# Routing and scattering tokens beside the attention, and running the experts over groups of 7, 7 and 2 batches in one pass

## The chip, the core and the metric

The kernel runs on one core of a Trainium2 chip. The metric is device time in microseconds, from one launch to its end. The core has five engines that work through queues of their own: TensorE (PE, matmuls and transposes), VectorE (DVE), ScalarE (ACT), GpSimd (POOL) and SyncE (SP, which here only issues DMAs). An engine executes its queue in order; semaphores make it wait for another engine or for a DMA.

## The reference

A transformer block over 16 batches of 512 tokens of width 128: causal attention with 16 heads of 8, and then a mixture of 160 experts of which every token uses 8. Each batch has its own shift, scale and gate vectors (`sa, ca, ga, sb, cb, gb`), and each half adds to the residual.

```python
mod = (silu(c) @ wmod).reshape(16, 6, 1, 128)
sa, ca, ga, sb, cb, gb = mod[:, 0], ..., mod[:, 5]
ga = sign(ga) * max(abs(ga), 0.25)          # gb likewise
h = layernorm(x) * (1 + ca) + sa
x = x + ga * attention(h)                   # qkv, rope, causal softmax, proj
h = layernorm(x) * (1 + cb) + sb
probs = sigmoid(h @ router_w.T + expert_bias)          # 160 experts
top_w, top_idx = top_k(probs, 8)
top_w = 2.5 * top_w / (sum(top_w) + 1e-9)
routed = sum over the 8: top_w * (silu(h @ w_gate[e].T) @ w_down[e].T)
shared = silu(h @ w_gate_shared.T) @ w_down_shared.T
x = x + gb * (routed + shared)
```

## The kernel before

All of `x` stays in SBUF. The work is done in two stages, one after the other.

**Attention** (`attention`). The 16 heads of a batch are handled in four groups of four, so there are 64 head groups, numbered `gg`. For every head group the scores are computed twice: once as queries by keys, for the row maxima (`maxima`: L317 and a mask matmul L324, then a DVE reduction L329 out of PSUM), and once as keys by queries, for the exponentials (`exponentials`: L363, L370, then ACT's `Exp` L373). A score tile holds two heads and takes two of PSUM's eight banks; there are three such tiles. `weighted` (L382) multiplies the exponentials with the values, and `collect` divides by their sum. The maxima of head group `gg + 2` are computed beside the exponentials of `gg`. `prepare(b)` makes queries and keys in a three-part bf16 form and writes them to DRAM (`parts`, L290); `fetch` reads them back into replicated form (L303, L306). `project` ends a batch and adds to `x`.

**Experts** (`experts`). The batches are taken in four groups of four. `route` normalizes a batch, computes the router's logits (L563), the top 8 (L581, L582), and the shared expert. `place` counts how many tokens go to each pair of experts, gives every (token, expert) a slot in blocks of 128 slots, and scatters the rows: for each 128 tokens, 8 indirect DMAs (L740, POOL) write the rows into `xg` in DRAM. With `NK = 8*16 + 79 = 207` blocks for each group there are 828 blocks in all. A `Quad` takes four blocks: `load` brings rows in, `turn` transposes them (L782, copied by DVE L784), `up` multiplies with the pair's gate weights (L790, then small DVE work, `Silu` on ACT L809 and a DVE product L812), `back` transposes (L819, copied by ACT L821), `down` multiplies with the down weights (L826, copied by ACT L834), and the result goes to `yg` in DRAM. `wd`, all the down weights, lies in SBUF. `combine` fetches the 8 results of each token again: 8 indirect DMAs for 128 tokens (L848, POOL), a DVE reduction (L858) and the product with the weight and gate (L859).

The rows of `xg` have to be zero before they are scattered to: 18 DMAs (L119) write zeros into two buffers of 207 blocks at the start, and four groups share the two buffers.

The order is set by generators: `compute` advances one step of `beside` after every quad. For group g these are the routing and placing of the later groups, and the `combine` of the group before. The framework's scheduler arranges the instructions of each engine.

```python
        for g in range(NGR):
            if g + 2 < NGR:
                groups.append(Group(g + 2))
                beside.append(arrive(groups[g + 2]))
            compute(groups[g], chain(*beside))
            beside = [chain(*(combine(groups[g], i) for i in range(GB_)))]
            if g + 2 < NGR:
                beside.append(place(groups[g + 2]))
        drain(chain(*beside))
```

Of the kernel before, what the change touches and what calls it, by code (L numbers as in the profile page):

```python
# [35 lines left out]
NGR = 4  # L36
GB_ = NB // NGR
TB = GB_ * NBLK
TOPK = 8

NK = TOPK * TB + NC - 1
FAR = 1e30
TINY = 1e-30
EPS = 1e-5
# [4 lines left out]
OFF = [sum(S - P * a for a in range(i)) for i in range(NBLK + 1)]  # L49
# [3 lines left out]
def block_kernel(ctx: ExitStack, tc: tile.TileContext, t: dict, out: bass.AP):  # L53
    nc = tc.nc

    const = ctx.enter_context(tc.tile_pool(name="const", bufs=1))

    stats = ctx.enter_context(tc.tile_pool(name="stats", bufs=4))
    early = ExitStack()
    early_pool = early.enter_context(tc.tile_pool(name="early", bufs=1))  # L60
# [7 lines left out]
    x = const.tile([P, NB * NBLK, D], FP, tag="x", name="x")  # L68

    def load_x(eng, b):  # L70
        eng.dma_start(
            out=x[:, b * NBLK : (b + 1) * NBLK, :],
            in_=t["x"][b].rearrange("(n p) d -> p n d", p=P),
        )

    load_x(nc.gpsimd, 0)
    cT = load("cT", [D, NB])
    wmod = load("wmod", [D, 6 * D], pool=early_pool)
    c = SimpleNamespace(
        ident=load("ident", [P, P]),  # L80
        wqk=load("wqk", [D, 2, 2, D], pool=early_pool),
        bqk=load("bqk", [D, 2, 2], pool=early_pool),
        wv=load("wvT", [D, D], pool=early_pool),
        bv=load("bv", [P, D], rows=True, pool=early_pool),
        turn=load("turn", [D, 2, S], pool=early_pool),
        identb=load("identb", [P, P], BF, pool=early_pool),
        mask_q=load("mask_q", [P, P], BF, pool=early_pool),
        mask_k=load("mask_k", [P, P], BF, pool=early_pool),
    )
    for b in range(1, NB):  # L90
        load_x(nc.sync if b % 2 else nc.gpsimd, b)
    c.wproj = load("wprojT", [D, D], pool=early_pool)
    c.bproj = load("bproj", [D, 1])
    c.wrout = load("wroutT", [D, E])
    c.bias_e = load("bias_e", [P, E], rows=True)
    c.wgs = load("wgsT", [D, I])
    c.wds = load("wdsT", [I, D])
    c.bias_p = load("bias_p", [NC, 2])
    c.onesb = load("onesb", [P, P], BF)
    c.ones = load("ones", [P, 1])  # L100
    c.earlier = load("earlier", [P, P], BF)
    c.pairs = load("pairs", [NC, 2, NC])
    c.spread = load("spread", [NC, 2, E])
    c.blocks = load("blocks", [P, NK])
    c.slots = load("slots", [P, NK])
    c.wg = const.tile([D, NC, P + 2], FP, tag="wg", name="wg")
    for k in range(8):
        sl = slice(k * NC // 8, (k + 1) * NC // 8)
        nc.gpsimd.dma_start(out=c.wg[:, sl, :], in_=t["wgT"][:, sl, :])


    xg = [tc.dram_tile([NK * P, D], FP, name=f"xg{i}") for i in range(2)]
    yg = [tc.dram_tile([NK * P, D], FP, name=f"yg{i}") for i in range(2)]
    zeros = early_pool.tile([P, 1, D], FP, tag="zeros", name="zeros")
    nc.gpsimd.memset(zeros, 0.0)
    for rows in xg:
        view = rows.rearrange("(p n) d -> p n d", p=P)
        for k in range(0, NK, 23):
            nc.sync.dma_start(out=view[:, k : k + 23, :], in_=zeros.broadcast_to([P, 23, D]))  # L119

    eps = const.tile([P, 1], FP, tag="eps", name="eps")
    nc.vector.memset(eps, EPS)


    mod = const.tile([D, 6, NB], FP, tag="mod", name="mod")
    with tc.tile_pool(name="pmod", bufs=1, space=PSUM) as pp, tc.tile_pool(
        name="smod", bufs=1
    ) as sp:
# [63 lines left out]
def attention(tc, c, x, mod, statistics, normalization):  # L192

    nc = tc.nc
# [808 lines left out]
```

## Time and profile before

| | |
|---|---|
| median of 3 runs | 3246.03 us (3240.66 to 3251.7) |
| the profiled execution's own time | 3244.43 us |
| its span, from first to last instruction | 3243.1 us |
| busy: PE, DVE, POOL, ACT | 1758.9, 1439.5, 1061.9, 906.9 us |
| PE's weight loads (beside the matmuls) | 1234.9 us |
| instructions | 37324 |
| mean granted clock of TensorE | 0.766 of full speed |
| DMA over the span | 277.55 MB, mean 86 GB/s |

The profile is of one execution. A row of its fifth part names a line of the kernel, the engine, what is written from what, how often, the busy time and the mean duration of one, and how long the engine was idle just before these instructions and what ended that. Part 2 cuts the span into 40 equal slices of 81 us and shows in tenths how busy each engine was; `PEclk` is the granted clock of TensorE in tenths. The windows view gives the same for stretches that one names, with the count of instructions in brackets. A matmul in fp32 is two instructions here; a transpose is one.

### The profile page before, as it was taken

Reading aid. Unit: us, or ns where it says so; the run is one execution under the profiler, and the core shown is the slowest. Engines: PE = TensorE matmul, PEld = TensorE weight load, DVE = VectorE, ACT = ScalarE, POOL = GpSimd, SP = SyncE. Lnnn points to the kernel's source line nnn. Section 1 sums busy time; section 2 is a strip of 40 time slices with the busy share of each in tenths; the row PEclk is TensorE's granted clock in tenths of the full one; section 3 lists DMA queues with packets and bytes.
Section 4 is the critical chain, followed back from the end, with each engine's and each line's share of the span. In section 5 each row is a group of like instructions: output and inputs, shape, how many; then the busy total and the mean of one; then the engine's idle time right before and its main releaser. Section 6 shows DMA issues by size and latency. Waiting matters only on the chain.

```text
span 3243.1 us, 37324 instructions
## 1 busy us (share of the span) xinstructions
PE 1758.9 (54%) x12772; PEld 1234.9 (38%) x12772; DVE 1439.5 (44%) x3719; ACT 906.9 (28%) x1448; POOL 1061.9 (33%) x1079
## 2 busy tenths in 40 slices
PE   2189889888988863141288235138137228336700
PEld 1044444444444432031187235137136117336600
DVE  4156666666766553140176344026336115235522
ACT  1044444544444441010055012015013004113400
POOL 3000000000000006726701664650662670662176
PEclk8589999999999965565599667559568569668855
DMA  9811111111111011111245234124234125334421
GB/s 285 232 53 48 58 52 46 59 52 48 52 59 50 31 65 43 51 57 60 71 140 151 71 94 120 55 77 127 54 90 134 62 68 157 82 93 132 136 58 49
DMA packets 348310, 277.55 MB, mean 86 GB/s; under 512 B 28032, under 2 KB 319584, under 8 KB 348128
## 3 DMA queue, kind: packets, MB, share of 16 engines
q1 hardware_dynamic: 313568, 200.56, 20.6%
q0 software_dynamic: 34560, 74.60, 8.0%
q8 instruction: 109, 1.79, 0.2%
q14 instruction: 73, 0.60, 0.1%
HBM read 142.54 MB, written 131.73 MB: 85 GB/s over the span
## 4 chain that ended last, share of the span: by engine, by line
PE 37%; another core or an unknown queue 20%; issue 13%; DVE 11%; ACT 7%; POOL 6%; SPq 4%; DMA 2%; ACTq 0%; DVEq 0%; POOLq 0%
PE av L382 8%; POOL got L848 6%; PE m L826 4%; PE u L790 4%; ACT pT L373 4%; PE s L317 4%; PE s L363 3%; PE m L819 3%; SPq L119 3%; PE m L782 2%; DVE s L858 2%; PE s L248 2%; DVE mins L329 1%; PE o L397 1%
## 5 line engine op out<-in xcount | busy, mean ns | idle before, releaser
L848 POOL DMA_INDIRECT got<-yg,idx x512 | 495.6, 968 | 668.9 <-DMA yg<-y 359.0
L740 POOL DMA_INDIRECT xg<-h,idx x512 | 500.1, 977 | 405.9 <-issue 152.6
L329 DVE TENSOR_REDUCE mins<-s 128x2 f32<-128x1024 f32 (+3 forms) x512 | 418.6, 820 | 316.7 <-PE s L324 309.0
L373 ACT ACTIVATE pT<-s 128x1024 f32<-128x1024 f32 (+3 forms) x512 | 357.3, 703 | 280.9 <-PE s L370 273.3
L790 PE MATMUL u<-wg,xT 128*128 x1656 | 261.9, 303 | 315.7 <-DVE xT L784 126.8
L819 PE MATMUL m<-ident,su 128*128 128x128 f32 x828 | 149.1, 310 | 417.6 <-DVE su L812 186.4
L790 PEld LDWEIGHTS u<-wg,xT 128*128 128x128 f32 x1656 | 234.7, 215 | 326.0 <-issue 234.2
L282 POOL TENSOR_TENSOR rot<-rot 128x1024 f32<-128x1024 f32 x16 | 37.7, 2353 | 931.5 <-DVE rot L257 931.5
L821 ACT COPY hwT<-m 128x512 f32<-128x512 f32 x208 | 121.5, 584 | 757.5 <-remote 439.3
L317 PE MATMUL s<-krep,qrep 96*128 96x512 bf16 (+3 forms) x1024 | 262.5, 308 | 105.5 <-DMA krep<-parts 92.4
L382 PE MATMUL av<-pT,v 128*32 128x256 f32 (+3 forms) x2048 | 276.2, 444 | 1.3 <-ACT pT L373 1.3
L819 PEld LDWEIGHTS m<-ident,su 128*128 128x128 f32 x828 | 105.1, 159 | 446.1 <-issue 386.1
L826 PE MATMUL m<-wd,hwT 128*128 x1656 | 255.3, 305 | 21.3 <-issue 20.3
L363 PE MATMUL s<-qrep,krep 128*128 128x512 bf16 (+3 forms) x1024 | 258.2, 306 | 12.1 <-DVE mins L329 11.9
L784 DVE COPY xT<-m 128x512 f32<-128x512 f32 x208 | 141.7, 682 | 237.6 <-remote 163.1
L826 PEld LDWEIGHTS m<-wd,hwT 128*128 128x128 f32 x1656 | 237.3, 221 | 23.0 <-issue 20.9
L858 DVE TENSOR_REDUCE s<-got 128x128 f32<-128x1024 f32 x64 | 120.9, 1889 | 245.4 <-DMA got<-yg,idx 242.3
L324 PE MATMUL s<-mask_q,identb 128*128 128x128 bf16 x1024 | 208.9, 223 | 0.0
L370 PE MATMUL s<-mask_k,identb 128*128 128x128 bf16 x1024 | 205.1, 221 | 0.0
L809 ACT ACTIVATE su<-u 128x520 f32<-128x520 f32 x208 | 125.8, 605 | 235.5 <-DVE zi L806 98.4
L834 ACT COPY y<-m 128x512 f32<-128x512 f32 x208 | 121.2, 582 | 213.8 <-issue 146.5
L782 PE MATMUL m<-ident,xs 128*128 128x128 f32 x828 | 145.5, 305 | 57.0 <-issue 22.9
(154 smaller groups left out, 2303.6 us busy)
## 6 DMA issues: line engine op xcount, KB each, us to landing
xs<-xg SPq DMA_DIRECT2D x204, 256.0 KB
yg<-y SPq DMA_DIRECT2D x204, 256.0 KB
xg<-zeros SPq DMA_DIRECT2D x18, 1472.0 KB
qrep<-parts SPq DMA_DIRECT2D x192, 96.0 KB
krep<-parts SPq DMA_DIRECT2D x192, 96.0 KB
parts<-three SPq DMA_DIRECT2D x16, 768.0 KB
xg<-h,idx POOLq DMA_INDIRECT x512
got<-yg,idx POOLq DMA_INDIRECT x512
```

The lines of the kernel that those rows point to most:

```text
L317: nc.tensor.matmul(sc[:, a, 0:n], lhsT=q[0:MROW, h, j * P : (j + 1) * P], rhs=k[0:MROW, h, 0:n], start=True, stop=False,)
L324: nc.tensor.matmul(sc[:, a, n - P : n], lhsT=c.identb, rhs=c.mask_q, start=False, stop=True)
L329: nc.vector.tensor_reduce(mins[gg][:, j, 2 * pr : 2 * pr + 2], sc[:, :, 0:n], AX.X, ALU.max, negate=True)
L363: nc.tensor.matmul(sc[:, a, 0:n], lhsT=k[:, h, i * P : (i + 1) * P], rhs=q[:, h, i * P : S], start=True, stop=False,)
L373: nc.scalar.activation(pT[:, 2 * pr : 2 * pr + 2, 0:n], sc[:, :, 0:n], AF.Exp, scale=SCALE)
L382: nc.tensor.matmul(av[HP * r : HP * (r + 1), i * P : S], lhsT=vs[b % 3][:, i, at : at + HP], rhs=pT[:, r, 0 : S - P * i], start=(i == 0), ...
L740: s = nc.gpsimd.indirect_dma_start(out=gr.xg[:, :], out_offset=bass.IndirectOffsetOnAxis(ap=gr.idx[:, j, k : k + 1], axis=0), in_=gr.h[:, ...
L782: nc.tensor.transpose(pt[:, j * P : (j + 1) * P], self.xs[:, j, :], c.ident)
L790: nc.tensor.matmul(pu[:, j, 0 : P + 2], lhsT=self.xT[:, j * P : (j + 1) * P], rhs=c.wg[:, bass.ds(self.pids[j], 1), :].rearrange("p o n -> ...
L819: nc.tensor.transpose(pt[:, j * P : (j + 1) * P], self.u[:, j, 0:P], c.ident)
L826: nc.tensor.matmul(py[:, j * D : (j + 1) * D], lhsT=self.hT[:, j * P : (j + 1) * P], rhs=wd[:, bass.ds(self.pids[j], 1), :].rearrange("p o ...
L848: nc.gpsimd.indirect_dma_start(out=got[:, k, :], out_offset=None, in_=gr.yg[:, :], in_offset=bass.IndirectOffsetOnAxis(ap=gr.idx[:, t0 + j ...
```

## The change

Routing, and for the first groups placing and scattering, is moved into the attention stage. In detail:

- **Groups** are 7, 7 and 2 batches. Each has its own `xg` and `yg`, and `32 * batches + 80` blocks: 304, 304 and 144, which is 752 blocks or 188 quads in place of 828 blocks or 208 quads. Every pair of experts gets at least one block.
- **Order.** PE, SP, ACT and DVE execute in source order (`manual_schedule`). A class `Steps` holds generators with a rank; in the attention every score tile or `weighted` is followed by a `tick`, which advances at most two of them, and each of them at most once in 3 ticks (`gap`); steps marked `"o"`, which use the single PSUM bank `o`, share that spacing among them. In the expert stage there is a tick for every quad and the gap is 1.
- **Attention.** Score tiles hold four heads where these are 256 columns or fewer. The order within a head group is the string `"emwemewmemewmewm"` (exponentials, maxima, weighted). `route` runs behind `project` of every batch, and `place` behind the last `route` of a group. `sigmoid` and the shared `silu` become `Exp` on ACT, then add 1 and `reciprocal` on DVE; the layer norm's root becomes `Ln` and `Exp`. The sum of the two rotated halves goes from POOL to DVE.
- **DRAM instead of SBUF.** `x` is fetched batch by batch; the normalized rows go to `rows`, the residual with the shared expert to `rest`, and both are read back. The zeros are written in pieces of 8 blocks, two after each head group, on SP.
- **Scatters.** `scatter_on` issues the 32 indirect DMAs of one batch, after every second head group, or every ninth quad. `in_order` keeps the DMAs in order by a small `memset` on POOL behind each batch of them.
- **Quads** of all groups follow in one run. The down weights come by a DMA per quad from DRAM, at an address that SP reads. `turn` is copied by ACT and `back` by DVE. A gather (8 indirect DMAs) is issued after every second quad when no scatter is left, and summed by DVE five gathers later (`LAG`) by three halving adds.

```diff
-NGR = 4
+GROUPS = (7, 7, 2)
+LAG = 5
+def slot_blocks(batches):
+    return TOPK * NBLK * batches + NC
+    ctx.enter_context(
+        tc.manual_schedule(engines={PE, SP, mybir.EngineType.Activation, mybir.EngineType.DVE})
+    )
...
+        def clear(self, k, n):
+            view = self.xg.rearrange("(p n) d -> p n d", p=P)
+            nc.sync.dma_start(out=view[:, k : k + n, :], in_=zeros.broadcast_to([P, n, D]))
...
+        nc.scalar.activation(prob, prob, AF.Exp, scale=-1.0)
+        yield
+        nc.vector.tensor_scalar(prob, prob, 1.0, None, ALU.add)
+        nc.vector.reciprocal(prob, prob)
...
+        nc.scalar.activation(us, ph, AF.Exp, scale=-1.0)
+        nc.vector.tensor_scalar(us, us, 1.0, None, ALU.add)
+        nc.vector.reciprocal(us, us)
+        nc.vector.tensor_tensor(us, us, ph, ALU.mult)
...
+    def in_order(transfers):
+        mark = nc.gpsimd.memset(fence, 0.0).ins
+        for i in transfers:
+            if fences:
+                tc.add_manual_dep(i, fences[-1].name, NO_SYNC, reason="order of issue")
+            tc.add_manual_dep(mark, i.name, NO_SYNC, reason="order of issue")
+        fences.append(mark)
+    def scatter(gr, i):
+        h = sb.tile([P, NBLK, D], FP, tag="hs", name="hs", bufs=3)
+        nc.sync.dma_start(out=h, in_=rows[gr.first + i])
+        yield
+        sent = []
+        for j in range(NBLK):
+            for k in range(TOPK):
+                s = nc.gpsimd.indirect_dma_start(
...
+        in_order(sent)
...
+            (p0,) = self.numbers(SP, 0, 1, NC - 4)
+            self.wd = moe.sb.tile([P, 4, D], FP, tag="wd", name="wd", bufs=7)
+            nc.sync.dma_start(out=self.wd, in_=t["wdT"][:, bass.ds(p0, 4), :])
...
+    def scatter_on():
+        if loaded:
+            drain(loaded.popleft())
+        if scatters:
+            loaded.append(scatters.popleft())
+            next(loaded[-1])
...
+    for gg in range(NGG):
+        b, g = divmod(gg, NG)
+        if g == 0 and b + 2 < NB:
+            steps.add(3, prepare(b + 2))
...
+        if gg + 1 < NGG:
+            steps.add(0, shift(gg + 1))
+        attend(gg)
+        for _ in range(2):
+            if clears:
+                gr, k, n = clears.popleft()
+                gr.clear(k, n)
+        if gg % 2:
+            scatter_on()
...
+    steps.gap, now.pairs = 1, 2
+    quads = [Quad(gr, q) for gr in groups for q in range(gr.nq)]
+    for i in range(-2, len(quads) + 5):
+        for stage, q in (
+            ("load", i + 2), ("turn", i), ("up", i - 1), ("back", i - 3), ("down", i - 4),
+        ):
+            if not 0 <= q < len(quads):
+                continue
+            quad = quads[q]
+            if stage == "load" and quad.q == 0:
+                while quad.gr.g not in placed:
+                    steps.tick()
+                while quad.gr.g and (scatters or loaded):
+                    scatter_on()
+            getattr(quad, stage)()
+            if stage == "down" and quad.q == quad.gr.nq - 1:
+                gathers.extend((quad.gr, k, j) for k in range(quad.gr.size) for j in range(NBLK))
+        steps.tick()
+        turn += 1
+        if scatters or loaded:
+            if turn % 9 == 0:
+                scatter_on()
+        elif gathers and turn % 2 == 0:
+            sums.append(gather(*gathers.popleft()))
+            if len(sums) > LAG:
+                combine(*sums.popleft())
+    while gathers or sums:
+        if gathers:
+            sums.append(gather(*gathers.popleft()))
+        if len(sums) > 2 or not gathers:
+            combine(*sums.popleft())
...
+    def tick(self, most=2):
+        self.now += 1
+        for s in list(self.all):
+            if most == 0:
+                break
+            if s[1] > self.now or (s[2] == "o" and self.free > self.now):
+                continue
+            if s[2] == "o":
+                self.free = self.now + self.gap
+            kind = next(s[3], self)
+            if kind is self:
+                self.all.remove(s)
+            else:
+                s[1:3] = self.now + self.gap, kind
+            most -= 1
```

## The prediction

> **What bounds the kernel now.** I read the page's slices first, then busy time by stretch, then POOL's timeline and the start of the chain of waits. The slices:
>
> ```profile
> PE   2189889888988863141288235138137228336700
> DVE  4156666666766553140176344026336115235522
> POOL 3000000000000006726701664650662670662176
> PEclk8589999999999965565599667559568569668855
> ```
>
> Three stages: a start without PE (two slices), attention with PE at 8 to 9 (to slice 15), and the experts, where PE is full only where POOL rests, and POOL stands at 6 or 7 where PE does not. By stretch:
>
> ```profile
> core 0: us, PE busy (x) PEld busy (x) DVE busy (x) ACT busy (x) POOL busy (x), PEclk, DMA share, GB/s
> 200.00:1135.00 935.00, 835.60 (x6719) 431.83 (x6716) 596.50 (x1140) 449.23 (x662) 30.62 (x13) 0.99 0.14 51
> ...
> 1640.00:1760.00 120.00, 115.01 (x958) 107.69 (x957) 96.69 (x354) 73.45 (x129) 0.00 (x0) 1.00 0.57 160
> 1760.00:2200.00 440.00, 155.53 (x1001) 143.28 (x1000) 141.69 (x411) 71.47 (x127) 248.24 (x257) 0.66 0.31 87
> ...
> 3060.00:3243.00 183.00, 0.49 (x5) 0.30 (x3) 38.39 (x36) 0.97 (x2) 123.42 (x128) 0.51 0.21 54
> ```
>
> Attention: PE is busy 89% of its time, DVE 64%. Experts without indirect DMAs: 958 PE instructions in 120 us, at 24 for a quad that is 3.0 us a quad. Beside indirect DMAs a group needs 440 us for some 42 quads, over 10 us each. The last 183 us are gathers alone. What one DMA costs POOL:
>
> ```profile
> 3120.10 0.95 POOL L848 DMA_INDIRECT got<-yg,idx  x1 [0.30 <-issue]
> 3121.36 0.95 POOL L848 DMA_INDIRECT got<-yg,idx  x1 [0.30 <-issue]
> ...
> 3149.04 1.43 POOL L848 DMA_INDIRECT got<-yg,idx  x1 [0.30 <-issue]
> ```
>
> 1.26 us from start to start, also where POOL has nothing else to do. The groups' means:
>
> ```profile
> L848 POOL DMA_INDIRECT got<-yg,idx x512 | 495.6, 968 | 668.9 <-DMA yg<-y 359.0
> L740 POOL DMA_INDIRECT xg<-h,idx x512 | 500.1, 977 | 405.9 <-issue 152.6
> ```
>
> With these means it is 1.28 us, so 1024 DMAs take 1310 us of POOL's queue, all after the attention, within some 2080 us. The rest of those is POOL waiting (359.0 us for `yg`), since routing, placing, quads and gathers of a group depend on each other. And the start:
>
> ```profile
> 123.91 5.24 SPq L119
> 129.26 10.25 DMA parts<-three
> ```
>
> The first queries and keys go out at 129 us, behind 18 clears of 5.24 us on SP; the first `Exp` begins 40 us later, at 169.
>
> **The change: the start.** Clears and 13 of the 16 loads of `x` leave the front. SP issues some 30 loads at 0.4 us (the chain shows 0.37 to 0.44 for small ones), and about 3 MB at the 284 GB/s of the first 50 us is 11 us. `prepare(0)` follows at its own pace, so `parts` should go out near 35 us, and the first head group start 40 us later: **75 us** in place of 169. The clears come back later: 752 blocks at 5.24 us per 23 are 171 us of DMA, 3.7 us in each of the first 47 head groups. Cover: the DMA share is 0.14 in attention and operands are fetched two head groups ahead. Were it gone, at most the 171 us come back.
>
> **The attention.** `prepare`'s first matmul recurs every 62 us (434.57, 496.50 in the chain), so the 935 us are 15.1 batches, each with 55.4 us of PE and 39.6 us of DVE. Added on PE, at attention's full-clock rates (0.164 us for 128 fp32 columns from L430, 10.5 us for 64; 0.478 for 512 from L248; 0.204 for a bf16 mask matmul): `route` has 18 instructions of 128 columns (2.95), 8 of 160 (1.6) and 2 of 512 (0.96), 5.5 us a batch, and 15 batches are routed inside the stage, 83 us. `place` of group 0 has 14 bf16 matmuls a batch, 20 us, and 5 around them. PE: 886 + 108 = 994 us. On DVE, by before's rows: the adds that POOL did (two of 0.69), statistics of `x` (4 of 0.28 and 0.17), less 1.3 saved by wider maxima tiles, +1.9 a batch. `route` by its rows 11.5 us. New are two reciprocals:
>
> ```profile
> L161 DVE RECIPROCAL stat<-stat 128x64 f32<-128x64 f32 x1 | 0.6, 553 | 2.0 <-ACT stat L160 2.0
> L600 DVE RECIPROCAL scale<-scale 128x4 f32<-128x4 f32 x16 | 2.8, 172 | 0.1
> ```
>
> That is 6.35 ns an element, so 4.2 us for 640 and 3.4 for 512. `route` is 19.1 us a batch, 287 for 15; `place` 4.4 a batch and 14 once, 45 us. DVE: 664 + 332 = 996 us. The removed table loads (1.28 us each) were on ACT in the experts' stage and are hidden behind POOL there; I count nothing.
>
> So PE and DVE have the same 995 us, each in source order and handing three score tiles to each other. Behind a 4.2 us reciprocal the next maxima reduction waits, and so PE's next tiles. Before, PE reached 886/992 = 89% beside a DVE at 64%. The trace has no stage with both full; bounds are 95% (1047 us) and 72% (1380). I take 85%, nearer to the row there is: **1170 us**, 18.3 a head group. A tie is broken either way by tens of us.
>
> **What is left for POOL.** I counted the ticks by the rule of `Steps`: `route` takes two head groups, and `place(0)` starts in head group 31. Its first scatter is issued at 41 and the seventh at 53; 41 us of POOL each against 36.6 us for two head groups, so all seven are done in the attention. `place(1)` starts at 59, and its first scatter comes only at quad turn 15 of the expert stage. So 9 of 16 batches of scatters and all gathers remain: 800 of 1024 DMAs.
>
> **The experts.** In the first 41 turns PE has also batch 15's routing and two placings (about 40 us) and DVE 75; with 3.0 and 2.3 us a quad that is 4 us a turn. Turn 15 comes 17 turns on, 62 us with arrival. From there POOL is never without work for long: each scatter batch is 32 of 1.28 and a fence (a memset on POOL took 0.22 to 0.25 us), 41.2 us, against 27 to 36 us for 9 turns. Nine are 371 us. Group 1 can load when its seven are in, at 62 + 288 = 350 us; its predecessor's quads are over at 42 * 4 + 34 * 3.05, some 270 to 285. So PE stands 65 us, and POOL goes on. Gathers begin at 433, 8 DMAs and a fence, 10.5 us, each for two turns of PE's 6.1. After five, DVE waits in `combine` for the gather, behind it the quads' DVE work and PE: 5.25 us a turn. Group 0's 28 end at 727; by then quads end within some 20 us (17 turns are free of gathers), where POOL waits. Then 36 gathers more. 64 * 10.5 = 672. Sum: 62 + 371 + 672 + 20 and 5 for the last sum and store, **1130 us**. The load of `wd` (256 KB a quad) beside `xs` and `y` brings DMA to 768 KB in 3.05 us, 252 GB/s against 285 seen; it could slow group 0, which has 65 us to spare. PE's extra register loads are covered by the same.
>
> Two rules of the Trainium skill speak against this. POOL's indirect DMAs beside a busy DVE: in the timeline a DVE product of two SBUF inputs (L812, 0.68 us at 1905.34) ran inside a DMA of 0.95, the slowest ones seen took 1.21 and 1.43, the mean is 0.97. "SBUF — State Buffer", section "A bandwidth-pool intuition that's wrong (but worth ruling out)", says that such a DMA is blocked until DVE's operation ends, 620 ns becoming 3100. By the row 800 DMAs are 1043 us with fences; by the rule, at 3.4 us from start to start, 2720. I take the row. And the clock: where POOL paced PE, 1760 to 2200, it was 0.66 and a quad took 3.7 us of PE (155.53 / 1001 * 24). "TensorE: Matmul & The Clock Gate", section "Part 1: The HAM clock gate", halves it after about 3.4 us of idling: 5.8 us a quad, over the 5.25 that gathers allow, and 54 turns would cost 30 us more. By the row nothing; I take that.
>
> Sum: 75 + 1170 + 1130 = 2375 us of span. The median of the runs shown is 2.9 above the span profiled, so **2380**.
>
> **The rivals.**
> - *PE and DVE lock step in attention* (0.20). The tie above, with in-order queues; for it, 4 us operations; against it, three score tiles and ACT's share. At 72%: 2590.
> - *POOL slower beside DVE, a little* (0.10). Half of the 800 at 1.43 instead of 0.95: +190, 2570.
> - *Attention nearly without stalls* (0.15). For it, few waits of PE on DVE now (11.9 us at L363). 95%, 1047: 2255.
> - *Scatters do not run beside the attention* (0.05), because SP, which has to bring the rows, is held up by clears and fetches. 7 * 41.2 more at the end: 2670.
> - *Slower than before* (0.03). The port lock by the rule above, at POOL. At S us per DMA the experts take 87 + 800 S, and the 224 early ones spill over once they need more than the 420 us from head group 41 on: 87 + 1024 S - 420. That reaches the 1998 us that are left at S = 2.28. At 3.4 the whole would be 4390.
> - The forecast holds the rest (0.47).
>
> **How the numbers follow.** A measurement of this kernel tells 0.3% from no change, 10 us. All cases but one are far below 3246; faster 0.96, same 0.01, slower 0.03. The range takes in the third rival down to 2190 (with a POOL that waits less) and the first two up to 2640; 2 in 10 lie outside.
>
> **What would show it.** First `Exp` near 75 us; head groups of 18 us with DVE and PE both at 80 to 90%; 224 scatters before some 1245 us and none between head group 53 and the experts; POOL at 7 to 8 tenths from 60 us into the experts to the end, a PE hole before group 1, a tail of 22 gathers, some 230 us, with PE idle. I am wrong if indirect DMAs grow beyond 1.1 us in the mean, if attention exceeds 1400 us, or if the experts end before 1000 us after attention, since POOL's count forbids it.

## The result, and the profile after

| | |
|---|---|
| before, in this comparison | 3244.99 us, median of 4 runs (3240.66 to 3251.7) |
| after | 3204.34 us, median of 4 runs (3193.91 to 3206.67) |
| ratio | 0.9867, 95% interval 0.9839 to 0.9894 |
| the profiled execution of after | 3206.67 us, span 3204.9 us, TensorE clock 0.750 |

The forecast was 2380 us. A gain of 1.3% came in place of 27%. The slices of the page of after, in the same rows as before:

```profile
PE   3877787878754445457854455444255458454300
DVE  4667767677844444448654443222144346343421
POOL 2000000000033333420033334555545540555575
PEclk8977878788877677779876778666577679677655
```

One slice is 80 us, and the first is slice 0. Scatters start in slice 11, beside the attention, as the change wants it: POOL shows 3 there. But PE falls from 7 or 8 to 4 in the same slices and DVE from 7 to 4, and both come back (slices 18 and 19: PE 7 and 8, POOL 0) as soon as POOL rests. From slice 20 on the experts repeat it: PE at 4 or 5, POOL at 3 to 5. Nothing is near 9. POOL's DMAs themselves cost what they did before:

```profile
L673 POOL DMA_INDIRECT xg<-hs,idx x512 | 497.4, 971 | 1691.0 <-DVE mins L302 867.1
L793 POOL DMA_INDIRECT got<-yg,idx x512 | 493.2, 963 | 469.2 <-issue 149.6
```

Before the means were 977 and 968 ns. So POOL is not slower beside a busy DVE; the others are slower beside POOL. Three stretches of 41 us show it (windows view: busy us of each engine and, in brackets, instructions; then clock, DMA share, GB/s). The first train of 32 scatters begins at 897 and ends at 938:

```profile
core 0: us, PE busy (x) PEld busy (x) DVE busy (x) ACT busy (x) POOL busy (x), PEclk, DMA share, GB/s
856.00:897.00 41.00, 27.18 (x218) 16.56 (x216) 34.88 (x78) 11.24 (x15) 0.00 (x0) 0.84 0.37 106
897.00:938.00 41.00, 17.72 (x97) 6.99 (x96) 9.37 (x23) 5.71 (x9) 31.07 (x33) 0.62 0.17 57
938.00:979.00 41.00, 32.04 (x232) 17.23 (x233) 26.40 (x52) 16.24 (x24) 3.92 (x4) 0.87 0.45 133
```

Beside the train PE executes 97 instructions, where it had 218 just before and 232 just after; DVE falls from 34.88 to 9.37 us of work. The timeline of the end of that train, each row with its start, its length, and in brackets the idle time before it and what ended it:

```profile
926.19 0.59 ACT L378 COPY aT<-o 128x512 f32<-128x512 f32 x1 [4.51 <-issue]
...
933.88 0.10 PEld L278 LDWEIGHTS <-qrep 96*128 96x128 bf16 x1 [2.67 <-issue]
934.10 0.96 POOL L673 DMA_INDIRECT xg<-hs,idx  x1 [0.31 <-issue]
935.28 0.26 PE L278 MATMUL s<-krep,qrep 96*128 96x128 bf16 x1 [2.22 <-issue]
935.36 0.96 POOL L673 DMA_INDIRECT xg<-hs,idx  x1 [0.30 <-issue]
935.98 0.10 PEld L285 LDWEIGHTS <-identb 128*128 128x128 bf16 x1 [2.00 <-issue]
936.63 0.96 POOL L673 DMA_INDIRECT xg<-hs,idx  x1 [0.30 <-issue]
937.38 0.26 PE L285 MATMUL s<-mask_q,identb 128*128 128x128 bf16 x1 [1.84 <-issue]
937.59 0.10 POOL L658 MEMSET fence<- 1x8 f32 x1
...
942.36 0.31 PE L278 MATMUL s<-krep,qrep 96*128 96x128 bf16 x1
942.36 1.23 DVE L288 TENSOR_REDUCE mins<-s 128x4 f32<-128x1024 f32 x1 [28.56 <-remote]
942.47 0.31 PE L285 MATMUL s<-mask_q,identb 128*128 128x128 bf16 x1
```

A matmul of 0.26 us starts every two microseconds, and what ended the idle time before it is "issue": there is nothing in the profile that PE waited for. ACT has such a gap too (4.51 us). DVE's 28.56 us are put down to "remote", an event whose sender the profile does not see; what it reduces there are the scores of the matmuls shown above it. Some 5 us after the last DMA of the train PE runs matmul on matmul again. I counted the starts of PE, DVE and ACT instructions (weight loads, semaphore waits and branches included) around the trains of more than 20 indirect DMAs in a row, per microsecond, by the time since the train's begin. The trains of 128 (the first and the last of before, the last of after) are not among them; with them the figures change little:

| us from the begin | 0 to 2.5 | 5 to 7.5 | 7.5 to 10 | 15 to 17.5 | 25 to 27.5 | 35 to 37.5 | 45 to 47.5 |
|---|---|---|---|---|---|---|---|
| after, 18 trains, mostly of 32 (40.5 us) | 15.5 | 14.9 | 9.6 | 5.0 | 1.8 | 0.7 | 10.5 |
| before, 19 trains | 14.0 | 12.2 | 7.4 | 5.6 | 2.4 | 3.1 | 4.2 |

The other engines go on for 7.5 us, or six DMAs, then fade within 20 us to almost nothing. SP, which issues the loads, fades with them: counted in the same way it starts 1.7 instructions per us at the beginning of a train of after and 0.04 from 35 to 37.5 us. In the kernel before the starts fade in the same way; I had taken its alternation of PE and POOL for dependencies.

By stages: the first `Exp` begins at 85 us, the last head group ends at 1591 us, and the experts take the other 1614 us. From the starts of the copies of `avs`, of which each head group has one, a head group takes 21.5 us up to number 40, 37.0 us from 41 to 53, beside the scatters, and 16.3 us after that. The last group of the first figure already stands beside the first train and takes 47.1 us; without it the figure is 20.8.

### The profile page after: what moved, and what is told of

It is laid out like the page before. It is cut to its first block, busy times and chain, and to the rows that moved or that the text cites. A ratio compares the mean times of both kernels' runs of the same rounds, so it can differ in the third digit from the quotient of the medians.

```text
span 3204.9 us, 37684 instructions
## 1 busy us (share of the span) xinstructions
PE 1792.2 (56%) x12424; PEld 1234.2 (39%) x12424; DVE 1574.8 (49%) x3805; ACT 839.6 (26%) x1327; POOL 1016.5 (32%) x1123
## 4 chain that ended last, share of the span: by engine, by line
PE 28%; DVE 25%; another core or an unknown queue 24%; issue 10%; ACT 5%; POOL 4%; DMA 2%; SPq 1%; ACTq 0%; DVEq 0%; POOLq 0%
DVE mins L288 4%; PE av L348 4%; POOL got L793 4%; PE s L327 3%; PE s L278 3%; PE down L760 3%; PE s L724 3%; PE s L210 2%; DVE su L745 2%; DVE hwT L755 2%; ACT su L742 2%; PE back L753 2%; DVE us L508 2%; PE turn L717 2%
## 5 line engine op out<-in xcount | busy, mean ns | idle before, releaser
L673 POOL DMA_INDIRECT xg<-hs,idx x512 | 497.4, 971 | 1691.0 <-DVE mins L302 867.1
L337 ACT ACTIVATE pT<-s 128x1024 f32<-128x1024 f32 (+2 forms) x384 | 336.7, 881 | 670.5 <-PE s L334 495.6
L760 PE MATMUL down<-wd,hwT 128*128 x1504 | 249.0, 319 | 165.8 <-issue 115.2
L753 PE MATMUL back<-ident,su 128*128 128x128 f32 x752 | 141.2, 318 | 355.6 <-DVE hwT L755 299.9
L278 PE MATMUL s<-krep,qrep 96*128 96x512 bf16 (+3 forms) x1024 | 281.1, 338 | 50.3 <-issue 19.9
L760 PEld LDWEIGHTS down<-wd,hwT 128*128 128x128 f32 x1504 | 226.8, 231 | 177.0 <-issue 122.2
L348 PE MATMUL av<-pT,v 128*32 128x512 f32 (+3 forms) x2048 | 247.2, 510 | 45.4 <-ACT pT L337 30.0
L742 ACT ACTIVATE su<-s 128x520 f32<-128x520 f32 x188 | 113.7, 605 | 508.6 <-DVE zi L740 347.9
L724 PE MATMUL s<-wg,xT 128*128 x1504 | 240.5, 311 | 5.1 <-issue 4.9
L724 PEld LDWEIGHTS s<-wg,xT 128*128 128x128 f32 x1504 | 224.8, 227 | 5.9 <-issue 5.9
L717 PE MATMUL turn<-ident,xs 128*128 128x128 f32 x752 | 141.9, 321 | 150.9 <-ACT xT L719 114.1
L278 PEld LDWEIGHTS <-qrep 96*128 96x128 bf16 x1024 | 108.7, 107 | 211.8 <-issue 179.8
```

Of the source, the lines that this page charges most:

```text
L278: nc.tensor.matmul(sc[:, a, 0:n], lhsT=q[0:MROW, h, j * P : (j + 1) * P], rhs=k[0:MROW, h, 0:n], start=True, stop=False,)
L337: nc.scalar.activation(pT[:, heads.start : heads.stop, 0:n], sc[:, :, 0:n], AF.Exp, scale=SCALE)
L348: nc.tensor.matmul(av[HP * r : HP * (r + 1), i * P : S], lhsT=vs[b % 3][:, i, at : at + HP], rhs=pT[:, r, 0 : S - P * i], start=(i == 0), ...
L673: s = nc.gpsimd.indirect_dma_start(out=gr.xg, out_offset=bass.IndirectOffsetOnAxis(ap=gr.idx[:, NBLK * i + j, k : k + 1], axis=0), in_=h[: ...
L717: nc.tensor.transpose(pt[:, j * P : (j + 1) * P], self.xs[:, j, :], c.ident)
L724: nc.tensor.matmul(pu[:, j, 0 : P + 2], lhsT=self.xT[:, j * P : (j + 1) * P], rhs=wg[:, bass.ds(self.pids[j], 1), :].rearrange("p o n -> p ...
```

## The experiments

Kernels that were tested together ran on one chip, beside the kernel before; which chip the first measurement had is not on record. The chips were of two kinds: on two of the four later ones (9 and 1) the kernel before takes 2958 us, on the other two (5 and 4) and in the first measurement 3245 to 3249 us. I call the first kind **free** and the second **held**, and give it with each time. Chip 9 was free both times that it was used, and each of the others was used once, so the name stands for what was seen beside the kernel before, and that it is a lasting property of a chip is not shown. After, e5, e6, e13, e16 and e17 are medians of 2 to 4 runs, the others single runs. The last columns are microseconds: head groups below are those up to number 40, from 41 to 53 (beside the scatters), and from 54 to 62; the end of the last head group; and from there to the end of the span. Where scatters hold, the first of these figures takes in one held group, as above: up to number 39 after and e5 both have 20.8.

| kernel | kind | before beside it | time | head groups | attention ends | experts |
|---|---|---|---|---|---|---|
| after | held | 3244.99 | 3204.34 | 21.5, 37.0, 16.3 | 1591 | 1614 |
| e10_as_it_is | held | 3248.11 | 3221.34 | 20.9, 37.3, 16.4 | 1578 | 1642 |
| e5_as_it_is | free | 2958.73 | 2489.96 | 20.6, 21.9, 16.5 | 1363 | 1133 |
| e1, e8 no_scatter | free | 2957.69, 2958.73 | 2394.88, 2394.48 | 20.6, 21.4, 16.4 | 1359, 1357 | |
| e2_memsets | free | 2957.69 | 2521.07 | 20.1, 24.1, 16.3 | 1372 | |
| e3, e14 direct | free | 2957.69, 2958.67 | 2411.47, 2395.99 | 20.6, 21.2, 16.2 (e3) | 1353, 1341 | |
| e18_direct | held | 3245.87 | 2676.55 | 20.6, 21.2, 16.3 | 1353 | 1322 |
| e4_spaced | free | 2957.69 | 2855.86 | 20.5, 25.1, 18.7 | 1428 | 1426 |
| e6_fours | free | 2958.73 | 2574.54 | 20.7, 25.4, 18.5 | 1439 | 1139 |
| e12_landed | held | 3248.11 | 2850.02 | 20.8, 28.6, 16.5 | 1458 | 1390 |
| e15_landed_fours | free | 2958.67 | 2909.05 | 20.0, 21.6, 16.3 | 1336 | 1571 |
| e7_no_reciprocal | free | 2958.73 | 2319.86 | 17.6, 19.6, 13.8 | 1192 | 1126 |
| e11_few_reciprocals | held | 3248.11 | 3100.91 | 18.6, 36.1, 14.3 | 1452 | 1647 |
| e16_few_reciprocals | held | 3245.87 | 3095.02 | 19.3, 35.7, 14.3 | 1472 | 1629 |
| e13_both | free | 2958.67 | 2586.46 | 18.3, 18.9, 14.4 | 1219 | 1367 |
| e17_both | held | 3245.87 | 2704.82 | 18.6, 27.0, 14.2 | 1331 | 1374 |

### The scatters left out, or replaced (e1, e2, e3)

Theory: trains of indirect DMAs hold the other engines. Rivals: any work of POOL does, or any DMA from its queue. The three edits in short form:

```diff
-                s = nc.gpsimd.indirect_dma_start(out=gr.xg, out_offset=..., in_=h[:, j, :], ...)
+                # e1: no DMA. e2: one copy, then nc.gpsimd.memset(busy, 0.0), 31 times
+                # e3: nc.gpsimd.dma_start(out=gr.xg[r : r + P, :], in_=h[:, j, :])
```

> Leaves out all 512 scatter DMAs; the slots stay zero. Theory 'starving': while POOL issues indirect DMAs one after another, the other engines start hardly anything (in the changed kernel 15 instructions per us before such a burst of 32, under 2 per us from 20 us into it), so POOL's time adds to theirs. Then head groups 41 to 53 take 19.7 us like the ones before them, the attention ends near 1360 us instead of 1600, and the experts lose 9 bursts of 40 us: about 2600 us in all. Rival 'order': the waits come from the source order of SP, DVE and PE (loads of the rows, placing, clears), which stay; then head groups 41 to 53 stay near 38 us and the whole is above 3000 us. Rival 'tie': DVE and PE hold each other up in attention whatever POOL does; head groups before and after 41 are the same, which both theories share, so it is read from the 19.7 us.

> Again without the 512 scatter DMAs, for the chip of this call. Head groups 41 to 53 at 21 us; the attention ends near 1360 us; the whole 2395 us if gathers run beside the quads as in the first call, near 2600 us if they hold them up here.

> Each scatter of 32 DMAs is replaced by one copy of 128 columns out of the loaded rows and 31 memsets of about 1.2 us on POOL; nothing is scattered. 'Starving' by the DMAs: POOL as busy as before but no harm, head groups 41 to 53 at about 20 us, whole about 2600 us plus at most the POOL time that nothing covers before the gathers, so 2600 to 2700. Rival 'busy POOL' (a port that POOL's work holds against VectorE): head groups at 38 us, whole near 3200 us.

> Each of the 512 scatter DMAs is replaced by a direct DMA of the same 64 KB from the same queue, POOL's, to 128 rows that follow each other. If it is POOL's making of descriptors as such that starves the others, head groups 41 to 53 stay near 38 us and the whole near 3200 us. If it is only the indirect form, near 2600 us.

All of these were far faster than the 3204 us, but the kernel before, run beside them, took only 2957.69 us (2958.73 beside e8). So none of this could be set against the first measurement; it needed the unchanged kernel on the same kind of chip. What stands by itself: memsets of 1.22 us on POOL lengthen a head group from 21.4 (e1) to 24.1 us (e2), so POOL's memsets are no neutral stand-in for DMAs.

### Pauses on POOL between the DMAs (e4)

```diff
-        in_order(sent)
+                in_order([s], busy)        # a memset of 1.2 us behind each DMA
```

(The comment is added, here and under e6, and the new argument of `in_order` is not shown.)

> Behind every scatter DMA POOL executes a memset of about 1.2 us, so that DMAs follow each other at 2.5 us instead of 1.27; gathers as they were. If each DMA costs the others its own time, whenever it comes, the attention ends near 1600 us as before, the experts some 0 to 350 us later since 9 bursts take 80 us: 3200 to 3550. If only a train of DMAs without pause starves the others (harm began 7.5 us into a burst), the head groups from 41 on stay near 20 us and the attention ends near 1400 us; the experts are then paced by POOL's 9 x 80 us, and the whole is 3000 to 3250 us.

2855.86 us on a free chip: every scatter now costs POOL 2.4 us in place of 1.26, and the experts' stage, which has 288 of them, grows to 1426 us. It says nothing on held chips.

### The kernel after, unchanged, on other chips (e5, e10) and the kernel before again (e9)

> The changed kernel with nothing edited, to stand beside the others on their chip, since the kernel before took 2958 us where the first four experiments ran and 3245 us where the change was measured. If the difference between the two is how much the indirect DMAs hold up the rest, the changed kernel differs as much or more: where before takes 3245 us it takes 3204 and head groups 41 to 53 take 37 us; where before takes 2958 us it takes 2700 to 2850 and those head groups 26 to 32 us. If the held-up rest is the same everywhere, head groups 41 to 53 take 37 us here too.

On a free chip after takes 2489.96 us, ratio 0.8417 (95% interval 0.8355 to 0.848). That is 110 us above the forecast time, though the gain is 16% in place of 27%, since before is faster there too, and it is below the 2700 to 2850 us expected of this run. The page and the stretches of that run:

```profile
PE   3787878778778787777887677774366768772000
DVE  4667766776678788767776777653265666772221
POOL 2000000000000047777100467777777773777776
PEclk8988787788789988888889899997778889995555
```

```profile
core 0: us, PE busy (x) PEld busy (x) DVE busy (x) ACT busy (x) POOL busy (x), PEclk, DMA share, GB/s
856.00:897.00 41.00, 27.11 (x216) 16.58 (x216) 34.87 (x78) 11.22 (x15) 0.00 (x0) 0.84 0.37 106
897.00:938.00 41.00, 34.51 (x277) 17.98 (x279) 31.74 (x69) 18.88 (x29) 31.33 (x32) 0.91 0.44 135
```

In the 41 us up to 897 both runs agree to within a tenth of a microsecond of work: PE 27.18 and 27.11, DVE 34.88 and 34.87. Then the same 32 DMAs start at the same time, and beside them PE executes 277 instructions here, 97 there. Before that point clock (0.84) and DMA rate (106 GB/s) are the same in both; they differ in what goes on beside the indirect DMAs of POOL. PE stands at 7 and POOL at 7 in the same slices.

> The kernel after, unchanged. Theory: 2490 us where the kernel before takes about 2960, 3200 where it takes about 3245, with trains of 32 indirect DMAs and PE nearly still beside them. Rival (the two times of the kernel after come from something that changes from run to run on one chip): 3200 beside a before of 2960, or the reverse.

> The kernel before, unchanged, with a profile on another chip. It took 3245 us where the change was first measured and 2958 us beside the later runs. Theory (on the first chip the other engines hardly start instructions while POOL issues a long train of indirect DMAs, on the others they go on): where it takes about 2960 us, attention ends near 1190 us as in the first profile, POOL's indirect DMAs stay at 0.97 us in the mean, and the whole difference lies after 1190 us, where PE is busy beside POOL. Rival (the first chip is slower throughout, in its clock or its memory): the attention of 200 to 900 us is shorter too, with less PE time. On a chip where it takes 3245 us the profile repeats the first one.

The next chip was a held one: 3221.34 us for after and 3249.09 us for before. The rival, that the time of after changes from run to run, falls: in all three comparisons it goes with the time of the kernel before beside it. The question where before saves its 287 us on a free chip was not answered, since its profile was taken on a held one only.

### Fewer DMAs in a row (e6)

```diff
+            for n in range(0, len(sent), 4):
+                in_order(sent[n : n + 4], busy)     # a memset of 4.6 us behind four
```

> Group 0's scatters go out in trains of 4 DMAs with a memset of about 4.9 us on POOL behind each; the rest is as in the changed kernel. If harm needs a train longer than some 6 DMAs (it began 7.5 us into one), head groups 41 to 53 take 21 to 25 us whatever the chip, and the attention ends 150 to 240 us earlier than in the changed kernel. If every DMA costs the others its time, the attention ends within 60 us of the changed kernel's.

2574.54 us on a free chip, ratio 0.8703 (0.8662 to 0.8744), slower than after unchanged there: the memsets cost DVE and PE (25.4 us a head group) where there was nothing to win.

### Waiting until the DMAs have landed (e12, e15)

POOL waits after every 8, or 4, indirect DMAs, scatters and gathers, until they have landed. This pauses the train without work on POOL.

```diff
-            tc.add_manual_dep(mark, i.name, NO_SYNC, reason="order of issue")
+            tc.add_manual_dep(mark, i.name, SYNC, reason="wait till it has landed")
...
-        in_order(sent)
+            in_order(sent[-TOPK:])
```

> POOL waits after every 8 indirect DMAs until they have landed. If POOL's queue is the bound of the experts' stage as forecast, 100 waits of about 2 us come on top there: some 2690 us where the kernel after takes 2490. Rival (the stage is bound by the quads): below 2560. On a chip like the first one: if the other engines stand still because DMAs pile up in POOL's queue, the pauses set them free, a head group beside scatters falls from 37 to about 22 us and the time from 3200 to below 2800; if they stand still because of the issuing itself, it stays at 3200 or rises.

On a held chip 2850.02 us beside 3221.34 for after: 371 us saved by adding waits. POOL's rows show what one costs:

```profile
931.64 0.96 POOL L674 DMA_INDIRECT xg<-hs,idx  x1 [0.30 <-issue]
934.01 0.09 POOL L659 MEMSET fence<- 1x8 f32 x1 [1.41 <-DMA xg<-hs,idx]
935.05 0.96 POOL L674 DMA_INDIRECT xg<-hs,idx  x1 [0.95 <-issue]
```

3.41 us from start to start in place of 1.26, so 2.2 us for eight. And what it brings, in stretches of the two kernels on the same chip, e10 first and then e12:

```profile
core 0: us, PE busy (x) PEld busy (x) DVE busy (x) ACT busy (x) POOL busy (x), PEclk, DMA share, GB/s
900.00:1300.00 400.00, 193.95 (x1279) 101.58 (x1290) 163.05 (x345) 81.41 (x120) 166.29 (x177) 0.70 0.28 86
1600.00:2800.00 1200.00, 586.38 (x3959) 534.85 (x3957) 445.04 (x1413) 273.80 (x487) 529.78 (x589) 0.72 0.45 139
```

```profile
core 0: us, PE busy (x) PEld busy (x) DVE busy (x) ACT busy (x) POOL busy (x), PEclk, DMA share, GB/s
900.00:1300.00 400.00, 263.95 (x1760) 139.81 (x1772) 232.08 (x479) 115.02 (x171) 218.79 (x251) 0.77 0.35 106
1600.00:2800.00 1200.00, 620.16 (x4072) 577.48 (x4070) 494.49 (x1519) 283.22 (x513) 713.64 (x804) 0.77 0.50 156
```

POOL gets more done in the second stretch (714 indirect DMAs in place of 548), although it now waits after each eight. The pauses do not set the others wholly free: a head group beside scatters takes 28.6 us, where I expected 22.

> POOL waits for landing after every 4 indirect DMAs in place of 8 (same function). Where before takes about 3245: in the trains of 32 the other engines go on for 7.5 us, some six DMAs, before they stop. If what stops them is the number that has piled up, trains of 4 never reach it: a head group beside scatters takes 22 to 24 us (28.6 with trains of 8), PE beside POOL as on the other chips, and the time is set by POOL, 1024 of 1.26 and 256 waits of 2.3 us with 340 us of PE's attention before: about 2700. If each DMA holds the others for its own time, the head groups stay at 28 us. Where before takes about 2960: about 2900, waits alone on top.

This one fell on a free chip, 2909.05 us: waits alone on top (200 of them in the experts, 1571 - 1133 = 438 us from e5, 2.2 us each), as expected there. Whether trains of four would be free of the hold on a held chip stays open.

### Direct DMAs on a held chip (e14, e18)

> The 512 scatter DMAs are direct ones of the same 64 KB from POOL's queue (leaves out where each row goes; output rows fall in other slots); gathers stay indirect. Where the kernel before takes about 3245 and a head group beside indirect scatters takes 37 us: if any DMA from POOL's queue holds the other engines, it stays above 30; if it takes the indirect kind with its 0.97 us of POOL each, it falls to about 21.5, and the time to some 2950 (240 us less in attention, the rest from the nine later batches). Where before takes about 2960 it repeats 2411 us and tells nothing new.

> Scatter DMAs direct (leaves out where each row goes). Where before takes about 3245: above 30 us a head group beside them if any DMA from POOL's queue holds the other engines, about 21.5 us and a time near 2950 if it takes the indirect kind. Where before takes about 2960 it repeats 2400 us.

e14 fell on a free chip (2395.99 us, nothing new), e18 on a held one: 2676.55 us, well under the 2950 expected, and a head group beside the DMAs takes 21.2 us, as on a free chip without any scatter (21.4). A direct DMA of the same 64 KB occupies POOL for 0.54 us, so a train of 32 lasts 17.3 us; with the indirect kind the others had faded to a third by then.

```profile
core 0: us, PE busy (x) PEld busy (x) DVE busy (x) ACT busy (x) POOL busy (x), PEclk, DMA share, GB/s
900.00:1300.00 400.00, 305.53 (x2482) 171.37 (x2479) 310.02 (x638) 158.33 (x229) 117.58 (x227) 0.89 0.39 120
```

2482 PE instructions in 400 us, against e10's 1279 in the same stretch above. So it is the indirect kind, not POOL's queue nor the bytes. What of that kind it is (POOL's 1.26 us for each, or rows that go to scattered places) was not separated. The gathers of this kernel are still indirect, and its experts' stage is held as ever: 1322 us, where e14 on a free chip takes 2394 - 1341 = 1053.

### The routing's reciprocals (e7, e11, e16)

On free chips 110 us were still missing against the forecast, in head groups without any indirect DMA. e7 leaves out the two adds and reciprocals of `route` (other experts are then chosen, and the shared expert's values differ). e11 and e16 keep the function: the 8 largest are picked before the sigmoid, which then has 32 values a row instead of 640, and ScalarE makes the shared expert's (`Ln`, then `Exp`). From the edit of e11 and e16:

```diff
-        nc.scalar.activation(prob, prob, AF.Exp, scale=-1.0)
-        nc.vector.tensor_scalar(prob, prob, 1.0, None, ALU.add)
-        nc.vector.reciprocal(prob, prob)
...
+        nc.scalar.activation(top, top, AF.Exp, scale=-1.0)
+        nc.vector.tensor_scalar(top, top, 1.0, None, ALU.add)
+        nc.vector.reciprocal(top, top)
...
-        nc.vector.tensor_scalar(us, us, 1.0, None, ALU.add)
-        nc.vector.reciprocal(us, us)
+        nc.scalar.activation(us, us, AF.Ln, bias=one[:I, :])
+        nc.scalar.activation(us, us, AF.Exp, scale=-1.0)
```

> Leaves out the two additions of 1 and the two reciprocals in routing, so that other experts are chosen; all other work stays. If DVE ties with PE in the attention (8.5 us of DVE a batch fewer), head groups up to 40 fall from about 20.6 to 19 us or less, and the attention is 80 to 130 us shorter. If PE alone sets that stage, they fall by less than 0.3 us.

> The eight largest are picked from the sums ahead of the sigmoid, and the sigmoid is taken of 32 values a row in place of 640; the shared expert's sigmoid is made by ScalarE (Ln, Exp). Same function. Theory (behind each 4 us reciprocal PE waits, so attention is longer than its busiest engine): DVE loses some 8 us a batch, a head group falls from 20.6 to about 17.6 us, attention ends near 1190 us, and the time is about 2320 us where the kernel before takes 2960; on a chip like the first one the trains then cost what they cost, about 3050. Rival (attention is set by PE alone): at most 1 us a head group, 2440.

> The few reciprocals alone, no waits. Where the kernel before takes about 2960: 20.6 - 2.3 = 18.3 us a head group, attention over near 1220 us, experts 1130 us as with the kernel after, 2350 us. Where it takes about 3245 it repeats 3101 us. Rival (what the routing saves comes back in the experts' stage): 2450 and over where before takes 2960.

e7 took 2319.86 us on a free chip: 170 us less than e5. DVE's busy time fell by 135 us in all, 2.1 us a head group, and a head group by 3.0 us: more than the work that was taken away, so other engines had been waiting behind it. e11 keeps the function and brings 20.9 - 18.6 = 2.3 us a head group and 120 us in all on a held chip; e16 is a repeat on another one, 3095.02 us, ratio 0.954 (0.9437 to 0.9644). PE's waits between 200 and 890 us, in e5 and then in e16 (total, times, longest):

```profile
PE o L360 <- ACT avs L880: 26.2, 14, 3.3
PE s L210 <- DVE rot L213: 22.6, 16, 2.3
PE o L513 <- DVE us L509: 22.6, 7, 3.2
PE s L327 <- DVE mins L288: 22.5, 14, 2.4
```

```profile
PE o L514 <- DVE us L510: 7.8, 9, 1.1
```

The wait for the shared expert's `us`, behind its 3.3 us reciprocal, falls from 22.6 to 7.8 us; of the others `avs` (25.8) and `rot` (23.7) stay near what they were, and `mins` falls to 17.3. How much e16 would take on a free chip was not measured.

### Both remedies (e13, e17)

> The few reciprocals and the waits for landing after every 8 indirect DMAs in one kernel (same function). Where the kernel before takes about 3245: the head groups before the scatters fall by the 2.3 us that the few reciprocals brought, 120 us in all, on top of the 2850 of the waits alone: about 2740. Where it takes about 2960, the waits only cost: 100 of 2.3 us on the 2320 that the same kernel without reciprocals took, about 2550. Rival (the waits bring nothing, the profile of the single run misled): 3100 and 2320.

> The few reciprocals and the waits after every 8. Where before takes about 2960 it repeats 2586 us, so the waits cost some 240 us against the few reciprocals alone. Where it takes about 3245: 2850 less some 120 us, 2740; rival: no better than 2850.

On a held chip they add up: 2704.82 us, ratio 0.8338 (0.8263 to 0.8412), the fastest version of the whole function there. On a free chip 2586.46 us, 0.8739 (0.8708 to 0.877): the waits cost more than the reciprocals save, and the kernel after as it is (0.8417) is better. With the waits the experts take 1374 us on a held chip and 1367 on a free one: the hold is gone from that stage. What is left of it is in the attention, 27.0 against 18.9 us a head group beside scatters, 13 * 8.1 = 105 us.

## Why the prediction was wrong, by its steps

**POOL's cost per DMA: right.** 1.28 us were taken and 971 and 963 ns of busy time came, with 0.30 between. The rule of the Trainium skill that was weighed against the row ("SBUF — State Buffer", section "A bandwidth-pool intuition that's wrong (but worth ruling out)"), a POOL DMA blocked until DVE is done, shows in no run: the means of the indirect DMAs are 956 to 1007 ns over all runs. The section measured it beside a DVE `tensor_copy`, and no run here was made to test that pair. The interference runs the other way on held chips, from POOL's DMAs to the others.

**The start: right in kind.** 85 us for the first `Exp` in place of 169; 75 had been predicted.

**The attention: 18.3 us a head group predicted, 20.6 measured without scatters (e1, e5), on held chips too as long as no train has begun.** The busy times were near (windows of e5, 200 to 900 us: PE 549.5 and DVE 510.9 of 700 us, so 16.2 and 15.0 us of 20.6; predicted 15.5 and 15.6). The mis-sized term is the share: 85% was taken, between 95 and 72, and 15.6 / 20.6 = 76% came. The rival of PE and DVE in lock step had the size. The two adds and reciprocals of `route` stand behind 3.0 us of a head group (e7), of which 2.1 are DVE's own time; whether it is the length of the reciprocals or the work alone that makes PE wait was not separated. PE's clock was 0.82 there, where rates from a stage at 0.99 had been used. On a free chip this is 1277 us from the first `Exp` to the end of attention, 107 more than the 1170 predicted.

**The experts, with POOL's queue back to back: right on free chips, wrong on held ones.** The steps that failed are "so all seven are done in the attention", which sets 41 us of POOL beside 36.6 us of the other engines, and "From there POOL is never without work for long". Both let PE, DVE and ACT go on beside POOL's DMAs and put the price to them at nothing. The experts' stage in the first measurement and then in e5, with the same PE instructions but for a few records:

```profile
1591.00:3205.00 1614.00, 717.78 (x4738) 652.29 (x4732) 594.79 (x1831) 336.46 (x596) 780.11 (x873) 0.70 0.43 132
```

```profile
1363.00:2496.00 1133.00, 622.25 (x4732) 574.81 (x4732) 591.58 (x1831) 332.68 (x596) 802.80 (x873) 0.82 0.59 188
```

1133 us on a free chip, against 1130 predicted, and the parts agree: the scatters end 434 us into the stage (433 predicted), the gathers of group 0 at 725 (727). Two runs of e5 lie 15 us apart, so an agreement to 3 us is in part luck. On the held chip POOL has 780 us of work in 1614: it waits for quads that could not run while it issued. The sum assumed of every DMA that PE, DVE and ACT go on beside it; in the held runs less and less goes on after the first 7.5 us, and nearly nothing from 25 us on. Of the 3205 - 2496 = 709 us between the two runs, 228 lie in the attention (seven trains, 33 us each) and 481 in the experts. So the 830 us between the 2375 of the sum and the first measurement are 10 at the start, 107 from the share in the attention, 228 and 481 from the hold, and a few that the experts' stage takes longer on free chips too, with rounding.

**The rivals.** None made POOL's DMAs stop the others. The one that was slower than before made the DMAs longer, which they did not become; scatters that do not run beside the attention would have cost 288 us; the hold costs 228 for the same seven trains, for another reason, and 481 more in the experts. Of the signs of being wrong one came, an attention of over 1400 us (1506). The rule on the clock that was weighed too would by estimate have made 5.8 us of PE a quad; by the prediction's own measure it was 3.6 (717.78 / 4738 * 24, clock 0.70) in the first measurement and 3.2 on a free chip (clock 0.82), and PE was not the bound. The clears, now beside attention, cost nothing that shows: in e5 PE's waits before L278, the first matmul on fetched operands, are 20.9 us in all, and 14.4 of them are one wait at the start.

At the held price the moved scatters gain little: a train beside the attention costs 33 of its 41 us.

**Could it have been read?** The stretch from 1760 to 2200 us of before has PE 155.53 and POOL 248.24 us busy of 440, together 92%, and its slices alternate. I put that down to dependencies. A timeline of one train of before would have told against it. PE ends the matmuls that write `m` at 1306.5; ACT, which has had nothing to do since 1302.8, copies `m` 33 us later, in the middle of a train of 128 scatters:

```profile
1304.82 1.65 PE L528 MATMUL m<-ident,mod 128*128 128x128 f32 x6
...
1339.34 0.37 ACT L537 COPY row<-m 128x256 f32<-128x256 f32 x1 [36.57 <-remote]
```

**What stays open.** Which resource the indirect DMAs take from the other engines was not found. The profile names "issue" and "remote" and no transfer that is late. Its records of DMA packets, in the first measurement, tell against two guesses. One is a late supply of instructions: their transfers have queues of their own there, and in the train at 897 two are seen, at 900.9 and 902.8 us, of 0.5 and 1.4 us; the next comes at 953.3, 11 us after PE runs again, and in 16 of the 18 trains none lies between 25 us and the return of PE. The other is a pile of DMAs that have not landed: the last packet of a train starts 0.9 to 1.3 us after POOL's last DMA ends, while in e5, where nothing is held, the train at 897 has 3.9. That it is the passing on of semaphores is argued from the word "remote" alone. Nor is it known what makes one chip held and another free, and shorter trains than 8 were not run on a held chip.

## What to carry to other kernels

Before moving DMAs of POOL beside other work, look at one train of them in the timeline: if the other engines' rows show "issue" or "remote" for tens of microseconds beside it, though their inputs are ready, the overlap that the sum counts on is not there. Long trains of indirect DMAs may want to be broken by waits until they have landed; here this gained 12% on one kind of chip and only added its 2.2 us per eight on the other, so measure on the chips that matter. When two engines with in-order queues are equally loaded, a share of 85% can be too much (76% here), and it pays to take the longest single instruction (a 4 us reciprocal of 640 values, of which 32 were needed) out first.

## What the runs showed of the hardware

- In the first measurement and on two of four later chips a train of indirect DMAs from POOL's queue lets PE, DVE and ACT start 15 instructions per us for 7.5 us, 5 at 15 us and 1 to 2 from 25 us on, and SP fades with them; in the train at 897 PE runs again 5 us after its end. On the other two they go on. Nothing else told the chips apart: in the 41 us before the first train two runs agree within a tenth of a microsecond of work (27.18 and 27.11 of PE).
- Direct DMAs of the same size from the same queue do no harm on the same kind of chip (21.2 us a head group, against 37).
- Waiting until eight have landed costs POOL 2.2 us and takes the hold out of the experts' stage (e17 and e13: 1374 us held, 1367 free; without the waits e16 has 1629 held).
- Memsets of 1.22 us on POOL cost the attention 2.7 us a head group (24.1 against 21.4, single runs), although no engine uses what they write.
